# Where batch 2's projection and batch 1's values stand in a gated cross-attention and mixture kernel

## The chip, the cores and the metric

The kernel runs on one core of a Trainium2 chip. The metric is device time in microseconds (us) of one execution of the whole program. A profiled execution leaves a page and a trace; its span is the time from its first to its last recorded instruction.

Each core has engines with queues of their own, each worked off in order: TensorE (PE, matrix products; its weight loads are shown as PEld), VectorE (DVE), ScalarE (ACT), GpSimd (POOL) and SyncE (SP), which here only issues DMAs. What one engine needs from another, it waits for on semaphores.

## The reference

Eight batches of 256 tokens with 512 features go through two blocks. All of it is float32.

```python
# x, ctx_2048: (8, 256, 512)
h = layernorm(x)
q = heads([ctx_2048, h] @ Wq, 32)          # 32 query heads of 16
k, v = heads(h @ Wk, 8), heads(h @ Wv, 8)  # 8 key and value heads
ks, vs = heads(ctx_2048 @ Wsk, 8), heads(ctx_2048 @ Wsv, 8)
scores = q @ [ks, k].T / 4 + alibi         # each of the two key halves:
scores[masked] = -inf                      # causal, the last 64 keys
x = x + tanh(g_xattn) * (softmax(scores) @ [vs, v] @ Wo)

t = layernorm(x)
probs = softmax(t @ w_router)              # 128 experts, the 4 best
basis[k] = silu(t @ w_gate[k]) * (t @ w_up[k])       # 8 bases of 256
mixed = sum over the 4 experts of their mix of the 8 bases
shared = (silu(t @ shared_w_gate) * (t @ shared_w_up)) @ shared_w_down
x = x + tanh(g_ffn) * (mixed @ w_down + shared)
```

## The kernel before

**Three kinds of work.** For each batch there are the projection, the attention with a tail for each of its two tiles of 128 tokens, and the feed-forward block. While the feed-forward of batch b runs, the attention of batch b + 1 and the projection of batch b + 2 run between its matmuls.

**The order is written by hand.** Each kind of work is a Python generator which emits some instructions and yields a cost. `start(gen, length, at, total)` enters one with a time at which it begins and the stretch over which its costs are spread. `run` (L1252) always continues the generator that is earliest by this clock. The clock exists only while the program is built: it settles in which order instructions enter each engine's queue. A unit of it is one batch. Batch 0's attention begins at -0.585, its feed-forward at about 0, the projection of batch 2 at -0.06 with a length of 0.62, that of batch b + 2 for the later b at b + 0.01 (L1265 to L1285).

**Projection.** `project(b)` (L507) loads the input `x` and the context (`ctT`, stored with features as rows) where b > 1, normalises on VectorE (`norm`), transposes the normalised tiles on PE (`tr_x`, result `xnT`), makes keys (`pk`, copied by ScalarE in four pieces to `kT`, L572), queries in four groups of eight matmuls (`pq`, four with `ctT`, four with `xnT`; each group copied to `qT` by ScalarE, L593), and values (`pv`, copied to `vpad` by `put_values`, L501). `pk`, `pq` and `pv` share one PSUM bank (`ps_one`, tag "one"), which a generator takes with `hold` and gives back with `give`. In `project(1)` the transposes go to another bank and no input is loaded, since it comes at the program's start.

**Values for the attention.** `diagonals(qd, eng)` (L491) issues four DMAs which copy a quarter of `vpad` to its place in `vbd`, the stationary operand of the value products (L731). There is one `vpad` and one `vbd` for all batches. Sixteen such DMAs make one batch's `vbd`. In `attention(b)` for b > 0 they go out on SP's queue at the steps `u` 1 and 2, mixed with the softmax.

**Attention.** A score group `i` (eight of them) has two softmax steps `u`. `score(i)` emits the score matmuls (L652), `soften` (L665) reads a block of scores on VectorE, adds the bias and finds the largest, `exponentials` (L684) is on ScalarE, `divide` (L693, L696) takes a reciprocal on VectorE and multiplies on GpSimd, `turn` (L709) transposes on VectorE, `values` (L731) multiplies with `vbd` on PE, `take` copies to `oT` on ScalarE. `tail(b, t, oT)` (L866) does the output projection (`po`), the sum with x and its norm, the transposes `tr_f`, the router (`pl`, the four best, `pst`, `pc`). The feed-forward of a batch begins when both tiles' `tr_f` are in `hT` and VectorE has formed sums of token tiles (`sT`).

**Batch 0's attention carries other work.** `first_batch` (L752) emits softmax and products of batch 0, and between them, by `piece(...)`, steps of a list of remaining projection work: `rest()` (L437) and behind it `project(1)`. A `piece` names the kinds of step which it may take: `BEFORE` and `MORE` are matmuls, `AFTER` is a copy out of PSUM. What is left at the end runs as `others()`.

**Feed-forward.** `feed_forward(b)` (L999) has ten pieces k: eight bases and two halves of the shared expert. Each is computed as seven block products of half size instead of eight (Strassen's way: sums of token tiles and of weight blocks), `m` at L1028 and L1037. The sums of weight blocks are formed once, in batch 0, by `sub` on VectorE and GpSimd, and written by `keep` to a scratch in HBM; later batches load them from there. For the pieces 0 to 2 this happens in `first_weights` (L269) and `first_sums`, before batch 0's feed-forward; for the pieces from 3 on inside its loop, one piece ahead. `after(i, g)` issues, when the last matmul that reads a weight buffer has been emitted, the load of the piece two further on. SP's queue carries all of these: weight loads, `vbd` copies, inputs and scratch writes, in the order in which they were emitted.

Of the kernel before, what the change touches and what calls it, by code (L numbers as in the profile page):

```python
# [15 lines left out]
P = 128  # L16
B, T, HID = 8, 256, 512
# [5 lines left out]
Q = 32  # L23
# [14 lines left out]
def gated_block(  # L38
# [23 lines left out]
    nc = tc.nc  # L62
# [45 lines left out]
    loaded = {}  # L108
# [160 lines left out]
    def first_weights():  # L269

        for k in (2, 0, 1):
            for g in range(1, 5):
                load_gu(k, g)
            if k == 2:
                yield 2.0
                later["wd"] = weight(w_down, I, HID, "wd", nc.sync)


                later["sd"] = sd = const.tile([P, NSI // 2, HID], F32, tag="sd", name="sd")
                nc.sync.dma_start(  # L280
                    sd, sw_down.rearrange("(j o p) n -> o p j n", o=2, p=P)[1]
                )
            if k == 0:
                yield 5.5
                yield from first_sums(2)
        yield 1.0
        yield from first_sums(0)
        yield 1.0
        yield from first_sums(1)
# [217 lines left out]
    def project(b, xns=None):  # L507
        def own():
            yield from hold(0.0 if b == 1 else GAP)

        def bank(shape, name):
            return ps_one.tile(shape, F32, tag="one", name=name)

        free = give
        if b > 1:
            while b > 2 and b - 3 not in stored:
                yield 0.5
            loaded[b] = load(b), load_context(b)
            yield 16.0
        xt, ctT = loaded[b]  # L520
        if xns is None:
            normed = norm(xt, range(NT), f"a{b}")
            yield 3.0
            xns = normed()
            yield 3.0
        xnT = two.tile([P, NC, T], F32, tag="xo", name=f"xnT_{b}")
        kT = two.tile([P, 2, 2, T], F32, tag="kT", name=f"kT_{b}")

        def keys(pk, s):
            w_sb, src = ((wsk_sb, ctT), (wk_sb, xnT))[s]  # L530
            for c in range(NC):
                nc.tensor.matmul(  # L532
                    pk[:, s, :], lhsT=w_sb[:, c, :], rhs=src[:, c, :],
                    start=(c == 0), stop=(c == NC - 1),
                )

        if b == 1:

            yield BEFORE
            yield from own()  # L540
            pk = bank([P, 2, T], f"pk_{b}")
            for t in range(NT):
                if t:
                    yield BEFORE
                    keys(pk, 0)
                    yield MORE
                evict = transposed(
                    xnT, xns[t], t, f"x{b}",
                    lambda shape, name: other_bank(2, name).rearrange("p (c n) -> p c n", n=P),
                )  # L550
                yield AFTER
                evict()
            yield BEFORE
            keys(pk, 1)
            yield AFTER
        else:
            for t in range(NT):
                yield from own()
                evict = transposed(xnT, xns[t], t, f"x{b}", bank)
                yield AFTER - 0.8  # L560
                evict()
                free()
                yield BEFORE + 0.8
            yield from own()
            pk = bank([P, 2, T], f"pk_{b}")
            for s in range(2):
                keys(pk, s)
                yield AFTER

        for par in range(2):  # L570
            for s in range(2):
                nc.scalar.activation(  # L572
                    kT[:, par, s, :], pk[:, s, :], AF.Copy, scale=kmask[:, par : par + 1],
                )
        free()
        yield BEFORE
        if b == 1:
            yield BEFORE


        qT = two.tile([P, NB, G, Q], F32, tag="qT", name=f"qT_{b}")
        for g in range(G):
            yield from own()
            pq = bank([P, T], f"pq_{b}_{g}")
            for c in range(2 * NC):
                nc.tensor.matmul(  # L586
                    pq, lhsT=wq_sb[:, c, g * P : (g + 1) * P],
                    rhs=(ctT if c < NC else xnT)[:, c % NC, :],
                    start=(c == 0), stop=(c == 2 * NC - 1),
                )  # L590
                if c % NC == NC - 1:
                    yield MORE if c < NC else AFTER
            nc.scalar.activation(  # L593
                qT[:, :, g, :], pq.rearrange("p (b q) -> p b q", q=Q), AF.Copy, scale=-0.25
            )
            free()
            yield BEFORE
        projected[b] = kT, qT


        yield from own()
        pv = bank([P, NT, 2, HK * D], f"pv_{b}")
        for t in range(NT):
            for s, (w_sb, src) in enumerate(((wsv_sb, ctT), (wv_sb, xnT))):
                for c in range(NC):
                    nc.tensor.matmul(  # L606
                        pv[:, t, s, :], lhsT=src[:, c, t * P : (t + 1) * P], rhs=w_sb[:, c, :],
                        start=(c == 0), stop=(c == NC - 1),
                    )
            yield AFTER if t else MORE  # L610
        put_values(pv)
        free()
        yield BEFORE


    def attention(b):
# [135 lines left out]
        def first_batch():  # L752

            scs = {0: score(0)}
            for u in range(2 * n + 3):
                i, j = divmod(u, 2)
                m = u // 4 - 1 if u >= 6 and u % 4 == 2 else None
                if m is not None:

                    into = scs.get(i - 1) or [bank(f"sc_{b}_{i}_{p}") for p in range(2)]  # L760
                    values(m, 0, pts[m], into)
                exponentials()
                if i < n:
                    nmax = memory(u)
                if m is None:
                    piece(BEFORE, MORE)
                yield 1.0
                for step, ps in enumerate(((2,), (3,), (0, 1))):
                    exponentials()
                    for p in ps:  # L770
                        if i < n:
                            soften(i, j, p, scs[i], prs[u], nmax, dens[u])
                    if step == 0 and m is not None:
                        values(m, 1, pts[m], into)
                        piece(BEFORE, MORE)
                    if step == 1:
                        if j == 1 and i + 1 < n:
                            assert i + 1 < n // 2 or "queries" in ready
                            if i + 1 in (3, 7):
                                piece(AFTER)  # L780
                                piece(BEFORE, MORE)
                            scs[i + 1] = score(i + 1)
                        if 0 <= u - 1 < 2 * n:
                            divide((u - 1) // 2, (u - 1) % 2, prs[u - 1], dens.pop(u - 1))
                    if step == 2:
                        if 0 <= u - 2 < 2 * n:
                            turn(u - 2)
                        if m is not None:
                            take(m, into)
                            if m == n // 4 - 1:  # L790
                                start(tail(b, 0, oT), 0.22, total=37.0)
                        piece(AFTER)
                    yield 1.0 if i < n else 0.3
            start(tail(b, 1, oT), 0.16, total=37.0)
            start(others(), 1.0, total=100.0)
            yield 0.1

# [7 lines left out]
        for u in range(2 * n + 4):  # L805
# [12 lines left out]
            yield 1.0  # L818

            for step, ps in enumerate(((2,), (3,), (0, 1))):  # L820
                if u in (1, 2) and step < 2:
                    diagonals(2 * (u - 1) + step, nc.sync)
                exponentials()
                for p in ps:
# [442 lines left out]
    start(after_diagonals(), 0.2, at=-0.535, total=1.0)  # L1267
    start(first_weights(), 0.39, at=-0.537, total=20.5)
    start(attention(1), 0.86, at=FIRST, total=74.1)
    at = -0.2  # L1270
    while 0 not in sides:
        at += 0.005
        run(at)
    for b in range(B):
        if b > 0:
            run(b + EARLY)
            if b + 1 < B:
                start(attention(b + 1), 0.86, at=b + EARLY, total=74.1)
            run(float(b))
            at = float(b)  # L1280
        start(feed_forward(b), b + 1.0 - at, at=at, total=72.9)
        if b + 2 < B:
            start(project(b + 2), 0.62, at=b + (0.01 if b > 0 else -0.06), total=60.0)
    run(float(B + 1))


# [37 lines left out]
```

## Time and profile before

| | |
|---|---|
| three timed runs | 1010.71, 1011.7, 1012.34 us; median 1011.7 |
| the profiled execution | 1013.49 us, span 1011.7 us, mean clock of PE 0.993 |
| HBM read and written | 158.87 MB, 14.68 MB |
| the chain that ended last | PE 86% of the span, DVE 5%, issue 2%, ACT 2%, POOL 2% |
| first feed-forward matmul of batch 0 | 88.9 us |

How to read it: the page gives busy time for each engine as a share of the span. "The chain that ended last" is followed back from the program's last instruction, at each step to what released it, and says on which engine the time lay. The table of waits names, for each kind of instruction of an engine, what ended the idle time before it: `PE sc L731 <- DVE nm L665: 5.3, 1, 5.3` is 5.3 us in total, one time, the longest 5.3, in which PE stood before a value product that VectorE's `soften` released. "issue" as releaser means that nothing which the profile shows was awaited. In a timeline a line is start and duration, engine, line of the kernel, operation, out<-in, shape, and in brackets the wait before it. Tables by window give for each stretch of time the busy time of PE, PEld, DVE, ACT and POOL with the number of instructions, and of SP, then the clock that PE was granted as a share of full speed, the busy share of the DMA engines and GB/s.

### The profile page before, as it was taken

Reading aid. Unit: us, or ns where it says so; the run is one execution under the profiler, and the core shown is the slowest. Engines: PE = TensorE matmul, PEld = TensorE weight load, DVE = VectorE, ACT = ScalarE, POOL = GpSimd, SP = SyncE. Lnnn points to the kernel's source line nnn. Section 1 sums busy time; section 2 is a strip of 40 time slices with the busy share of each in tenths; the row PEclk is TensorE's granted clock in tenths of the full one; section 3 lists DMA queues with packets and bytes.
Section 4 is the critical chain, followed back from the end, with each engine's and each line's share of the span. In section 5 each row is a group of like instructions: output and inputs, shape, how many; then the busy total and the mean of one; then the engine's idle time right before and its main releaser. Section 6 shows DMA issues by size and latency. Waiting matters only on the chain.

```text
span 1011.7 us, 27844 instructions
## 1 busy us (share of the span) xinstructions
PE 985.7 (97%) x10470; PEld 797.3 (79%) x10470; DVE 601.8 (59%) x2241; ACT 441.6 (44%) x1657; POOL 471.6 (47%) x892
## 2 busy tenths in 40 slices
PE   8899799899999999999999999999999999999998
PEld 8777687768888687886778868797788868787885
DVE  2775767467553685536755467645756466665453
ACT  3754444246442564325543356423554245442231
POOL 4783676536542363423634246432455325651341
PEclk9999899999999999999999999999999999999999
DMA  6945744689354784457745586446954468665891
GB/s 208 219 171 155 224 152 129 185 216 304 124 164 144 208 288 142 147 166 217 249 127 158 167 256 216 135 137 190 276 188 140 150 181 260 201 192 167 281 301 64
DMA packets 117302, 192.15 MB, mean 190 GB/s; under 512 B 12848, under 2 KB 34864, under 8 KB 117168
## 3 DMA queue, kind: packets, MB, share of 16 engines
q1 hardware_dynamic: 112672, 184.87, 59.6%
q10 hardware_dynamic: 4112, 4.46, 1.3%
q8 instruction: 83, 1.36, 0.6%
q0 software_dynamic: 384, 1.05, 0.5%
q14 instruction: 51, 0.42, 0.1%
HBM read 158.87 MB, written 14.68 MB: 172 GB/s over the span
## 4 chain that ended last, share of the span: by engine, by line
PE 86%; DVE 5%; issue 2%; ACT 2%; POOL 2%; DMA 1%; SPq 1%; ACTq 0%; DVEq 0%; POOLq 0%
PE m L1028 39%; PE m L1037 10%; PE pq L586 8%; PE sc L731 6%; PE po L893 5%; PE sc L652 5%; PE pd L1171 4%; PE pk L532 2%; PE pv L606 2%; PE pd L1174 2%; PE pl L923 1%; DVE pr L665 1%; ACT pr L684 1%; PE tr_x L204 1%; SPq L496 1%
## 5 line engine op out<-in xcount | busy, mean ns | idle before, releaser
L696 POOL TENSOR_SCALAR pr<-pr,rd 128x192 f32<-128x192 f32 (+2 forms) x512 | 212.1, 434 | 243.9 <-DVE rd L693 226.8
L684 ACT ACTIVATE pr<-pr,nm 128x192 f32<-128x192 f32 (+2 forms) x512 | 219.0, 431 | 106.7 <-DVE nm L665 55.3
L1028 PE MATMUL m<-w,sT 128*128 128x256 f32 x1024 | 252.3, 380 | 1.3 <-issue 0.8
L1028 PEld LDWEIGHTS m<-w,sT 128*128 128x128 f32 x1024 | 193.6, 190 | 28.9 <-issue 1.5
L665 DVE CUSTOM_DVE_ANT_1 pr<-sc,nbias 128x192 f32<-128x192 f32 (+2 forms) x512 | 153.7, 321 | 98.0 <-PE sc L652 91.1
L1028 PE MATMUL m<-w,hT 128*128 128x256 f32 x768 | 203.8, 388 | 1.0 <-DVE u L1073 1.0
L1028 PEld LDWEIGHTS m<-w,hT 128*128 128x128 f32 x768 | 139.6, 191 | 25.6 <-issue 6.3
L1118 POOL TENSOR_TENSOR mixed<-mixed,th 128x256 f32<-128x256 f32 x112 | 81.5, 728 | 137.5 <-DVE th L1113 137.5
L709 DVE STREAM_TRANSPOSE pt<-pr 128x768 f32<-128x768 f32 (+2 forms) x128 | 111.4, 870 | 3.8 <-POOL pr L696 3.1
L684 ACT ACTIVATION_READ_ACCUMULATOR pr<-pr,nm 128x1 f32 x512 | 98.0, 191 | 0.0
L1074 POOL TENSOR_TENSOR m<-m,u 128x256 f32<-128x256 f32 x80 | 61.4, 768 | 67.3 <-DVE u L1073 58.5
L990 ACT ACTIVATE th<-m 128x256 f32<-128x256 f32 x80 | 30.7, 384 | 138.5 <-DVE up L1084 138.4
L731 PEld LDWEIGHTS sc<-pt,vbd 64*32 64x32 f32 x5120 | 60.6, 106 | 25.8 <-issue 14.2
L731 PE MATMUL sc<-pt,vbd 64*32 64x64 f32 (+2 forms) x5120 | 68.2, 228 | 8.9 <-DVE nm L665 5.3
L1096 DVE TENSOR_TENSOR gate<-u,m 128x256 f32<-128x256 f32 x80 | 33.2, 416 | 72.0 <-PE m L1028 66.5
L1084 DVE TENSOR_TENSOR up<-u,m 128x256 f32<-128x256 f32 x80 | 33.3, 416 | 67.9 <-PE m L1028 41.1
L990 ACT ACTIVATE th<-gate 128x256 f32<-128x256 f32 x80 | 33.3, 416 | 76.5 <-DVE gate L1096 76.5
L652 PE MATMUL sc<-kT,qT 32*128 32x192 f32 (+2 forms) x1024 | 63.6, 336 | 2.8 <-DVE nm L665 2.5
L1037 PE MATMUL m<-sT,w 128*128 128x128 f32 x512 | 66.2, 278 | 0.0
L652 PEld LDWEIGHTS sc<-kT,qT 32*128 32x128 f32 x1024 | 44.3, 184 | 26.5 <-issue 7.1
L1037 PEld LDWEIGHTS m<-sT,w 128*128 128x128 f32 x512 | 62.3, 194 | 0.4
L1171 PE MATMUL pd<-sd,shT 128*128 128x512 f32 x128 | 61.5, 603 | 0.2 <-DVE shT L1107 0.2
(131 smaller groups left out, 1376.0 us busy)
## 6 DMA issues: line engine op xcount, KB each, us to landing
w<-s SPq DMA_DIRECT2D x284, 256.0 KB, 3.5
w<-in_L_ffn_w_gate SPq DMA_DIRECT2D x130, 256.0 KB, 3.1
w<-in_L_ffn_w_up SPq DMA_DIRECT2D x73, 256.0 KB, 4.1
vbd<-vpad SPq DMA_DIRECT2D x120, 128.0 KB, 3.1
s<-w SPq DMA_DIRECT2D x40, 256.0 KB, 3.3
w<-in_L_ffn_shared_w_gate SPq DMA_DIRECT2D x32, 256.0 KB, 2.9
w<-in_L_ffn_shared_w_up SPq DMA_DIRECT2D x18, 256.0 KB, 3.8
sd<-in_L_ffn_shared_w_down SPq DMA_DIRECT2D x16, 256.0 KB, 3.5
```

Source lines behind the costliest of these rows:

```text
L586: nc.tensor.matmul(pq, lhsT=wq_sb[:, c, g * P : (g + 1) * P], rhs=(ctT if c < NC else xnT)[:, c % NC, :], start=(c == 0), stop=(c == 2 * N ...
L652: nc.tensor.matmul(seen(scs[p][:, j * COLS : (j + 1) * COLS], qb), lhsT=qT[rows, qb].rearrange("p g q -> p (g q)"), rhs=kT[rows, par, :, f ...
L665: nc.vector.tensor_tensor_reduce(out=part, in0=seen(scs[p][:, j * COLS : (j + 1) * COLS], qb0 + j), in1=bass.AP(tensor=bias.tensor, offset ...
L684: nc.scalar.activation(part, part, AF.Exp, bias=nmax, scale=-1.0, accum_out=den)
L696: nc.gpsimd.tensor_scalar(part, part, rden[:, p : p + 1], 1.0, op0=ALU.mult, op1=ALU.mult)
L709: nc.vector.transpose(pt[:, u % 4].rearrange("p c (s k) -> p (c s) k", s=2)[:, :, lo:], pr.rearrange("p c (s k) -> p (c s) k", s=2)[:, :, ...
L731: nc.tensor.matmul(scs[gp][32 * c : 32 * (c + 1), 2 * COLS + lo * Q : 2 * COLS + hi * Q], lhsT=vbd[rows, kb % (P // Q), kb // (P // Q) * 2 ...
L990: nc.scalar.activation(th, gate, AF.Tanh, scale=0.5)
L1028: nc.tensor.matmul(dst, lhsT=sides_of[m][c], rhs=w[:, c, :], start=(first and c == 0), stop=(c == NC // 2 - 1), skip_group_check=True,)
L1037: nc.tensor.matmul(dst[:, cols], lhsT=w[:, c, cols], rhs=sides_of[m][c], start=(first and ic == c == 0), stop=(c == NC // 2 - 1), skip_gro ...
L1118: nc.gpsimd.tensor_add(mixed[t], mixed[t], th)
L1171: nc.tensor.matmul(po, lhsT=shT[:, ic, t * P : (t + 1) * P], rhs=down[ic], **flags)
```

## The change

Six edits, of which none adds or removes a computation:

- `first_weights` loads batch 2's `x` and `ctT`, behind the weight loads of its last piece. `project(2)` then doesn't load them.
- The values of a batch become a function of their own, `project_values`. For batch 1 it is called ahead of the queries, for later batches behind them, as before.
- `first_batch` takes no `piece` of matmuls at step 9.
- Batch 1's sixteen `vbd` copies are issued on SP at the end of `first_batch`, in place of steps 1 and 2 of `attention(1)`.
- `project(2)` starts at -0.2 with a length of 0.75 (before: at -0.06, 0.62).
- The loop no longer starts `project(2)`; the projections of batches 3 to 7 start as before.

```diff
@@ first_weights
             if k == 0:
                 yield 5.5
                 yield from first_sums(2)
+        loaded[2] = load(2), load_context(2)
         yield 1.0
         yield from first_sums(0)
@@ project
         if b > 1:
             while b > 2 and b - 3 not in stored:
                 yield 0.5
-            loaded[b] = load(b), load_context(b)
-            yield 16.0
+            if b not in loaded:
+                loaded[b] = load(b), load_context(b)
+                yield 12.0
+            yield 4.0
         xt, ctT = loaded[b]
...
         yield BEFORE
         if b == 1:
             yield BEFORE
+            yield from project_values(b, ctT, xnT, bank, own, free)
+            ready.add("values")
...
         projected[b] = kT, qT
+        if b > 1:
+            yield from project_values(b, ctT, xnT, bank, own, free)
+
+    def project_values(b, ctT, xnT, bank, own, free):
         yield from own()
         pv = bank([P, NT, 2, HK * D], f"pv_{b}")
         for t in range(NT):
...
         put_values(pv)
         free()
         yield BEFORE
@@ first_batch
                 if i < n:
                     nmax = memory(u)
-                if m is None:
+                if m is None and u != 9:
                     piece(BEFORE, MORE)
...
             start(tail(b, 1, oT), 0.16, total=37.0)
+            assert "values" in ready
+            for qd in range(P // Q):
+                diagonals(qd, nc.sync)
             start(others(), 1.0, total=100.0)
@@ attention, batches from 1 on
             for step, ps in enumerate(((2,), (3,), (0, 1))):
-                if u in (1, 2) and step < 2:
+                if b > 1 and u in (1, 2) and step < 2:
                     diagonals(2 * (u - 1) + step, nc.sync)
@@ the schedule
     start(attention(1), 0.86, at=FIRST, total=74.1)
+    start(project(2), 0.75, at=-0.2, total=60.0)
     at = -0.2
     while 0 not in sides:
...
         start(feed_forward(b), b + 1.0 - at, at=at, total=72.9)
-        if b + 2 < B:
-            start(project(b + 2), 0.62, at=b + (0.01 if b > 0 else -0.06), total=60.0)
+        if 0 < b < B - 2:
+            start(project(b + 2), 0.62, at=b + 0.01, total=60.0)
```

## The prediction

> **What bounds the kernel now.** I read the engines' busy time first, then who TensorE waited for, then the clock by window, then the timeline around each wait.
>
> ```profile
> PE 985.7 (97%) x10470; PEld 797.3 (79%) x10470; DVE 601.8 (59%) x2241; ACT 441.6 (44%) x1657; POOL 471.6 (47%) x892
> ```
>
> TensorE (PE) is busy 985.7 of 1011.7 us, and the change neither adds nor removes a matmul. Only PE's idle time and time at half clock can move. The instruction orders of the two programs differ from batch 0's second half of attention to the end of batch 0's feed-forward (about 43 to 225 us) and nowhere later, so only waits before 225 us count. They are, in that view (us in total, times, longest):
>
> ```profile
> PE sc L731 <- DVE nm L665: 5.3, 1, 5.3
> PE sc L731 <- issue: 3.3, 1, 3.3
> PE pk L532 <- ACT xnT L205: 1.8, 1, 1.8
> ...
> PE pq L586 <- ACT kT L572: 0.8, 1, 0.8
> ...
> PE m L1028 <- DMA w<-in_L_ffn_w_up: 0.5, 1, 0.5
> PE pq L586 <- ACT qT L593: 0.5, 1, 0.5
> ```
>
> The clock comes on top. In the table by windows (the first figure after the window's length is PE's busy time, PEclk is near the end) a window with PE busy for 47% or less is followed by one at 0.50, one at 60% is not:
>
> ```profile
> 41.54:44.95 3.41, 1.59 (x22) 1.13 (x22) 3.27 (x15) 3.19 (x14) 2.86 (x8) 1.00 0.95 220
> 44.95:48.37 3.42, 3.42 (x8) 2.29 (x8) 2.26 (x11) 1.57 (x8) 3.42 (x8) 0.50 1.13 217
> ...
> 188.30:191.73 3.43, 2.06 (x89) 1.42 (x75) 2.30 (x11) 0.19 (x1) 2.29 (x4) 1.00 0.97 244
> 191.73:195.14 3.41, 1.50 (x45) 1.46 (x46) 1.42 (x3) 0.66 (x3) 0.73 (x1) 1.00 0.38 141
> 195.14:198.55 3.41, 3.41 (x18) 3.41 (x18) 0.94 (x2) 0.54 (x2) 0.44 (x1) 0.50 0.51 153
> ```
>
> So a hole of some 1.8 us in one window costs up to 1.7 us more (3.41 at half).
>
> **What the change takes away.** Before, SP issues twelve of the sixteen `vbd` copies, `x` and `ctT` between 91.69 and 103.6, ahead of the first weights of piece 3. These start at 103.67, land late, and VectorE, which must subtract them, stands still with batch 1's softmax queued behind it:
>
> ```profile
> 103.67 0.47 SPq L349 DMA_DIRECT2D w<-in_L_ffn_w_gate  x1
> ...
> 111.97 0.69 DVE L980 TENSOR_TENSOR w<-w,w 128x512 f32<-128x512 f32 x1 [3.27 <-DMA w<-in_L_ffn_w_gate]
> ...
> 117.01 1.55 PE L731 MATMUL sc<-pt,vbd 64*32 64x96 f32 x64 [5.25 <-DVE nm L665]
> ```
>
> Afterwards these eighteen DMAs are issued earlier: `x`, `ctT` behind the loads of piece 1 (some 59 us, while the queues are under 40% busy from 60 to 80 us), the copies from the end of batch 0's last value products on, 16 at about 0.64 = 10 us of SP, before piece 2's reload needs SP. Piece 3's loads then leave as soon as piece 1's matmuls free their buffers, and batch 2's projection (21 us of PE work) stands between pieces 0 and 5, so PE has work while VectorE subtracts. Gone: 5.25 + 0.48, and half clock from 117.0 to 120.05, 1.5: **-7.2**. The 0.8 before `pq` at 134 us shrinks, since two more groups cover `kT`: between -0.8 and 0, nearest -0.5.
>
> The 3.28 us "issue" hole at 190.36 lies inside a run of equal matmuls and waits for no engine; a 16 KB packet of the instruction queue moved at 191.4, among 380 GB/s of other traffic. With its half-clock window (195.14 to 198.55) it costs 3.28 + 1.7 = 5.0. It stands at a fixed place in PE's stream, in the second half of batch 1's last value products. In the new order about 1.8 us of other matmuls (two runs of L1037) come between the halves instead of 0.9. Bounds: it stays (0) or goes (-5.0); nearer to going, as twice the cover is there: **-3.6**. The Trainium skill (Runtime: NRT & Kernel Launch, Instruction fetch mechanics) says that crossing a 16 KiB block of instructions is mostly hidden; this hole was not, and by the rule the term would be -5.0.
>
> **What it adds.** Batch 0 first. `u` counts softmax steps, two to a score group. (1) The key matmuls `pk<-xnT` move behind score group 5 and the value products. Gone are 1.82 of wait and the half-clock 3.68 against 1.73 for eight such matmuls. But group 5's banks are free only when VectorE has read step 9's first two blocks (45.4), and the value products need the transpose that ends at 47.3: PE idles 2.3 + 1.1, with 0.5 of half clock. `pk` ends at about 51.0; the same work was done before at 50.8: **+0.2** (up to +1.7 if the clock falls twice).
>
> (2) The hole that decides. ScalarE's order is now exp 10 (two), `oT`, the four `kT` copies, exp 10 (two). The last wait for `kT`, hence for `pk` at 51.0: 1.6 + 1.0 + 0.1 = 53.7, and VectorE's reciprocal of step 10 with all behind it waits there, as it did at 53.19 before:
>
> ```profile
> 53.19 0.17 DVE L693 RECIPROCAL rd<-dn 128x4 f32<-128x4 f32 x1
> ...
> 62.09 0.34 DVE L665 CUSTOM_DVE_ANT_1 pr<-sc,nbias 128x192 f32<-128x192 f32 x1
> ...
> 63.12 0.93 PE L652 MATMUL sc<-kT,qT 32*128 32x192 f32 x16
> ```
>
> From there to step 13's first block VectorE worked without a break for 8.9 us; its order is unchanged, so step 13 begins at 62.6. Before, PE had three halves of query products to do meanwhile (57.0 to 63.1). Now it has `po` (3.4), score 6 (0.9) and `pv` (3.6), done at 59.0; then come `pq<-ctT` in the one bank that `pv` holds. The copy of `pv` to `vpad` stands on ScalarE behind the first exp of step 13: 62.6 + 0.4 + 0.7 + 0.6 = 64.4. PE idles 5.4 us (5.0 to 5.5), with score 7 and the rest of batch 0 queued behind it, and starts at half clock: 4.4 us of it on the windows above, 2.0 lost (1.7 to 3.4). **+7.4**.
>
> (3) Three times a second query group follows the first with nothing between, at 0.47 each (the row of `pq <- qT`), once before: **+0.9** (0.5 to 1.4).
>
> (4) From `po` of the second tile to `tr_f` VectorE and GpSimd need 4.1 us (82.42 to 86.55); PE now has 2.15 to do in it: idle 1.95 against 1.66 before (0.73 + 0.26 + 0.67): +0.3. In one piece it may cost a window: 0 or 1.7, the middle 0.8. **+1.1**.
>
> (5) VectorE has batch 2's norm (two statistics 1.8, two normalisations 1.4 to 2.9) in the same order, behind `xn_f` and ahead of the router's top-4. `rest`, which `pst` of tile 1 transposes, is then ready some 8.1 us after `xn_f`; PE is there after 2.4 (`tr_f`, score, `pl`) + 3.5 = 5.9, and all matmuls of piece 0 queue behind: 2.3 (1.9 to 2.8) and a window of 0 to 1.7, taken at 1.0. **+3.3**.
>
> (6) Without projection, pieces 5 to 7 have 11.1 + 8.6 + 8.1 = 27.8 us of PE work by the rows' durations, against 28.4 on VectorE and 28.3 on GpSimd. Before, projection filled them. Piece 6 alone lacks 1.3. Bounds 0 (batch 1's piece 2 ran in 7.27 us with VectorE busy 6.97) and 3.2; taken **+1.6**.
>
> The Trainium skill (TensorE: Matmul & The Clock Gate, Why this matters for your kernels) warns of PE gaps over about 3 us only. The windows above show half clock after gaps of 1.8 and 1.9. By the rule the 0.8 and 1.0 of (4) and (5) fall away, and the sum would be 1.8 less.
>
> Sum: 0.2 + 7.4 + 0.9 + 1.1 + 3.3 + 1.6 = 14.5 added; 7.2 + 0.5 + 3.6 = 11.3 removed: **+3.2 us**. The profiled execution took 1013.49 with a span of 1011.7; the timed runs' median is 1011.7 too, so the sum is put on that: 1014.9.
>
> **The rivals.** *The early hole is not there*: the softmax runs ahead by the 2.1 us that group 5 starts earlier, and `vpad` is copied before PE needs it. For: VectorE waited 2.10 for group 5 at 49.37. Against: `kT` on ScalarE. Then (2) falls: 3.2 - 7.4 = -4.2, 1007.5; with the fetch hole quite gone 1006. Chance 0.31. *All cancels*: fetch hole gone (-1.4), no half window in (4) and (5) (-1.8), (6) hidden (-1.6): -1.6, 1010.1. Chance 0.18. *The late pieces bind too*: fetch hole stays (+3.6), (6) at 3.2 (+1.6): +8.4, 1020. Chance 0.12. *The 111 us stall stays*, since VectorE had 29.5 us of work for PE's 25 there, and not the loads alone bound it: +7.2, 1022. Against: PE's pieces 1 to 3 grow to 38.5 us of work. Chance 0.04.
>
> **Numbers.** The forecast itself has 0.35, its own range 1013 to 1019. Slower by over 0.2% (2.0 us, about what a measurement of this kernel can tell from no change): 0.35 + 0.12 + 0.04 = 0.51. Within: 0.18. Faster: 0.31. The range takes in the first rival to 1006 and the third at 1020.
>
> **What would show it.** Right: PE idle some 5 us before `pq<-ctT` near 59 us, released by ScalarE's `vpad`; a PE wait of 2 us at `pst` on VectorE's `rest`; piece 0's first matmul some 9.6 us later than 88.87; no wait on a weight's DMA near 120; few idle gaps to 180. Wrong: first feed-forward matmul before 93, or the hole under 2 us; then the first rival holds. A hole in pieces 5 to 7 over 4 us, or a stay of the fetch hole, makes it worse than 1019.

## The result and the profile after

The changed kernel's four timed runs took 1016.51 to 1018.71 us, median 1017.89; four of the kernel before took 1010.71 to 1012.34, median 1011.91. The ratio is 1.0071, 95% interval 1.005 to 1.0092: slower, by about 6 us. The profiled execution of the changed kernel took 1016.51 us with a span of 1014.7.

The two profiled spans are only 3.0 us apart. The first trace of before is one of its longer executions: a second one (run e1) has a span of 1008.9. All programs here are the same up to batch 1's first key products. These begin at 39.65 in the first trace of before, at 38.45 in the second and at 38.41 in that of after, so the readings below are against the second: +5.8 us of span from an equal start.

First the page's line of busy time of the changed kernel, then who TensorE waited for from 40 to 232 us, that is to the end of batch 0's feed-forward (us in total, times, longest).

```profile
PE 984.0 (97%) x10470; PEld 795.3 (78%) x10470; DVE 598.3 (59%) x2241; ACT 441.8 (44%) x1657; POOL 471.4 (46%) x892
```

```profile
PE pq L591 <- ACT vpad L503: 3.9, 1, 3.9
PE tr_f L204 <- DVE xn_f L190: 3.2, 2, 2.2
PE sc L661 <- DVE nm L674: 2.6, 3, 1.9
PE pst L969 <- DVE tsum L963: 2.2, 2, 1.9
PE sc L740 <- DVE pt L718: 1.9, 2, 1.6
PE m L1040 <- ACT prob L946: 1.6, 1, 1.6
PE sc L740 <- issue: 1.5, 1, 1.5
PE pq L591 <- ACT qT L598: 1.4, 3, 0.5
```

The work is the same. The two long waits of before (5.3 near 112 us, 3.3 without a releaser near 190) are gone, and the eight kinds above stand in their place. Batch 0's first feed-forward product, in the second trace of before and in after:

```profile
86.33 1.03 PE L1028 MATMUL m<-w,hT 128*128 128x256 f32 x4
```

```profile
97.43 1.03 PE L1040 MATMUL m<-w,hT 128*128 128x256 f32 x4
```

From the first key products to this product after takes 97.43 - 38.41 = 59.0 us, before 86.33 - 38.45 = 47.9, so **+11.1**. From there to batch 1's first feed-forward product it takes 133.5 against 138.3: **-4.8**. The rest, 783.8 against 784.3, has the same order of instructions. Against the first trace, from which the prediction was worked out, the two stretches are +9.8 and -4.2 (49.2 and 137.6 there).

### The profile page after: what moved, and what is told of

The parts are those of the page before. It is cut to its first block, busy times and chain, and to the rows that moved or that the text cites. A ratio compares the mean times of both kernels' runs of the same rounds, so it can differ in the third digit from the quotient of the medians.

```text
span 1014.7 us, 27827 instructions
## 1 busy us (share of the span) xinstructions
PE 984.0 (97%) x10470; PEld 795.3 (78%) x10470; DVE 598.3 (59%) x2241; ACT 441.8 (44%) x1657; POOL 471.4 (46%) x892
## 4 chain that ended last, share of the span: by engine, by line
PE 85%; DVE 6%; DMA 3%; SPq 2%; ACT 1%; POOL 1%; issue 1%; ACTq 0%; DVEq 0%; POOLq 0%
PE m L1040 37%; PE pq L591 10%; PE m L1049 9%; PE sc L740 6%; PE po L905 5%; PE sc L661 5%; PE pd L1183 4%; PE pv L615 2%; PE pk L535 2%; PE pd L1186 2%; DMA x<-in_x 1%; SPq L497 1%; DMA wo<-in_L_xattn_Wo 1%; DVE pr L674 1%; PE pl L935 1%
## 5 line engine op out<-in xcount | busy, mean ns | idle before, releaser
L740 PE MATMUL sc<-pt,vbd 64*32 64x96 f32 (+2 forms) x5120 | 68.5, 229 | 3.7 <-DVE pt L718 1.9
```

The costliest lines, as they stand in the source:

```text
L740: nc.tensor.matmul(scs[gp][32 * c : 32 * (c + 1), 2 * COLS + lo * Q : 2 * COLS + hi * Q], lhsT=vbd[rows, kb % (P // Q), kb // (P // Q) * 2 ...
```

## The experiments

The last two columns are those two stretches in the profiled execution. Their sum follows the ratios roughly, and they say where a run gained or lost. They are of one execution: that of e9 took 1008.19 us, 2 below its median. In brackets is the median of the kernel before in the same comparison.

| run | median us | ratio to before, 95% | to first feed-forward product | batch 0's feed-forward |
|---|---|---|---|---|
| e1 before again | 1010.95 (1011.33) | 1.0003, 0.9986 to 1.002 | 47.9 | 138.3 |
| e2 early loads only | 1009.53 (1011.33) | 0.9983, 0.9967 to 0.9999 | 47.7 | 136.3 |
| after | 1017.89 (1011.91) | 1.0071, 1.005 to 1.0092 | 59.0 | 133.5 |
| e3 projection 2 late | 1016.92 (1011.33) | 1.0067, 1.0043 to 1.0091 | 59.4 | 132.0 |
| e4 values in one piece | 1010.22 (1011.33) | 0.9992, 0.9977 to 1.0006 | 51.7 | 133.9 |
| e5 copy one place earlier | 1013.98 (1011.2) | 1.0033, 1.002 to 1.0047 | 55.4 | 132.8 |
| e6 no skip at step 9 | 1009.17 (1011.2) | 0.9981, 0.997 to 0.9992 | 51.0 | 132.6 |
| e7 = e4, length 0.88 | 1006.16 (1011.2) | 0.9956, 0.9941 to 0.9972 | 51.2 | 130.1 |
| e8 = e4 and e6 | 1021.62 (1011.2) | 1.0097, 1.0073 to 1.012 | 58.5 | 137.9 |
| e9 = e6, projection 2 late | 1010.31 (1010.25) | 1.0, 0.9984 to 1.0016 | 51.0 | 132.2 |
| e10 = e6, length 0.88 | 1004.94 (1010.25) | 0.9954, 0.9939 to 0.9969 | 50.5 | 129.3 |
| e11 = e6, length 1.0 | 1006.74 (1010.25) | 0.9966, 0.9953 to 0.9979 | 51.2 | 130.7 |
| e12 = e10, vbd late | 1005.84 (1011.74) | 0.9945, 0.9924 to 0.9965 | 50.8 | 130.9 |

**e1, the kernel before once more.** No edit.

> The kernel before, once more, for a second trace. If the hole of 3.28 us without a releaser in the value products at 190 us belongs to that place in TensorE's stream, it is there again, with 1 to 4 us, and the time is 1011.9 within 0.1%. If it is chance, it is absent, and the span is 3 to 5 us below the 1011.7 of the first trace. The wait of 5.25 us near 112 is there in both cases.

The hole near 190 came again, with 2.72 us at the same matmul (37 of a run of 64 left), and the wait near 112 with 5.20. So the hole belongs to the place. What differed was the clock: a window at half clock at 45 us, which only the first trace has, and behind the hole two such windows in the second trace against one.

**e2, the early loads alone**, on the kernel before.

```diff
+        loaded[2] = load(2), load_context(2)
         yield 1.0
         yield from first_sums(0)
...
-            loaded[b] = load(b), load_context(b)
+            if b not in loaded:
+                loaded[b] = load(b), load_context(b)
             yield 16.0
```

> Before, with batch 2's x and ctT issued on SP some 40 us earlier, and no other instruction moved. My theory: the weights of piece 3 come late because twelve vbd copies stand ahead of them, and x and ctT are only the last two of fourteen; they move up by about 1.3 us, the wait near 112 shrinks from 5.25 to about 4, the time to 1010 to 1011.5. Rival: the two inputs' own traffic (1 MB) is what delays them: then the wait is under 1 us and the time 1004 to 1007.

The wait near 112 fell from 5.20 to 3.90: about the two DMAs' time on SP (102.35 to 103.67 in before), 2 of the 14 that stand ahead of the weights. The inputs' traffic is not the cause.

**e3, batch 2's projection at its old place**, on after.

```diff
-                yield 12.0
-            yield 4.0
+            yield 16.0
...
-    start(project(2), 0.75, at=-0.2, total=60.0)
...
-        if 0 < b < B - 2:
-            start(project(b + 2), 0.62, at=b + 0.01, total=60.0)
+        if b + 2 < B:
+            start(project(b + 2), 0.62, at=b + (0.01 if b > 0 else -0.06), total=60.0)
```

> After, but batch 2's projection starts where it did before; its early loads, the values ahead and the early vbd copies stay. My theory: the early vbd copies remove the wait near 112, and the early projection causes the new waits of TensorE at pieces 0 and 5 to 8 (1.6 before a feed-forward product at 101, 1.0, 0.2, 1.9 and 1.6 from 176 to 200). So the early hole of 3.9 stays, the 112 wait stays away, the late ones go: 6 to 7 us below after, 1010.5 to 1012. Rival: the projection's matmuls in pieces 0 to 5 are what covers VectorE's lag near 112; then a wait of 3 to 5 us comes back there and the time is 1015 to 1018.

Both were half right. The waits at 101 and from 176 to 200 shrank to 0.7 and less, but one of 1.61 came at 119 with a half-clock window behind it, and 0.8, 0.74 and 0.67 elsewhere. The stretch is 132.0 against 133.5, the time not measurably different from after. So the loss of 11 us in the first stretch has nothing to do with the early projection.

**e4, both tiles' value products in one piece**, on after.

```diff
-            yield AFTER if t else MORE
+            if t:
+                yield AFTER
+            elif b > 1:
+                yield MORE
         put_values(pv)
```

> After, but both tiles' value products of batch 1 in one piece, so that their copy stands on ScalarE between the exponentials of step 12, and not behind the first of step 13. My theory: the copy is done at about 59.4 instead of 62.6, TensorE's wait before the first query products falls from 3.9 to under 1, no half clock follows (1.7), the first feed-forward product comes at about 92.6 instead of 97.4, and of these 4.8 us VectorE's lag in pieces 5 to 8 takes 1 to 2 back: 1013.5 to 1015.5. Rival: VectorE and GpSimd set the end of batch 0's feed-forward; then all is given back, and the time stays at 1017 to 1018.

The wait fell from 3.86 to 0.68, the first stretch by 7.4 us, and only 0.4 of it came back later. The time fell by more than my theory said, since everything behind `pv` in the list moved up by one place: the three waits of 0.47 before query groups vanished too, and that before `tr_f` fell from 2.17 to 0.88.

**e5, the copy alone.** To separate the hole from that, one ScalarE instruction is moved by one place.

```diff
                 for step, ps in enumerate(((2,), (3,), (0, 1))):
+                    if u == 13 and step == 1:
+                        piece(AFTER)
                     exponentials()
```

> After, with one ScalarE instruction moved by one place: the copy of batch 1's values stands ahead of the first exponential of step 13 and not behind it; no other instruction moves on any engine. My theory: the copy then waits for the exponentials of step 12 only, which end at 60.1; TensorE's wait before the first query products falls from 3.9 to 1.9, and the time by 2, or by 3.4 if the half clock after it goes too: 1014 to 1016. Rival: the wait is paid again by the softmax chain behind it (VectorE idles 4.1 before score group 7 anyway): time unchanged at 1017 to 1018.5.

Timelines of after around the hole (start, duration, engine, line, operation; the wait before it in brackets), TensorE first, then ScalarE:

```profile
57.73 1.06 PE L615 MATMUL pv<-wv,xnT 128*128 128x128 f32 x8
62.65 1.67 PE L591 MATMUL pq<-ctT,wq 128*128 128x256 f32 x4 [3.86 <-ACT vpad L503]
```

```profile
59.99 0.19 ACT L693 ACTIVATION_READ_ACCUMULATOR pr<-pr,nm 128x1 f32 x1
61.43 0.45 ACT L693 ACTIVATE pr<-pr,nm 128x192 f32<-128x192 f32 x1 [1.25 <-DVE nm L674]
...
62.02 0.58 ACT L503 COPY vpad<-pv 128x512 f32<-128x512 f32 x1
```

and ScalarE and TensorE in e5:

```profile
60.33 0.18 ACT L693 ACTIVATION_READ_ACCUMULATOR pr<-pr,nm 128x1 f32 x1
60.42 0.56 ACT L503 COPY vpad<-pv 128x512 f32<-128x512 f32 x1
61.77 0.45 ACT L693 ACTIVATE pr<-pr,nm 128x192 f32<-128x192 f32 x1 [0.79 <-DVE nm L674]
```

```profile
61.04 1.99 PE L591 MATMUL pq<-ctT,wq 128*128 128x256 f32 x8 [1.90 <-ACT vpad L503]
```

The products were done at 58.8. ScalarE was free at 60.2 but stood before an exponential whose largest score VectorE had not found; the copy could have run then. One place earlier the wait is 1.90, as expected to a tenth, the half clock behind it is gone, and so are 3.9 us of the time. The wait was not paid again.

**e6, the skip at step 9 undone**, on after.

```diff
-                if m is None and u != 9:
+                if m is None:
                     piece(BEFORE, MORE)
```

> After, but with the piece at step 9, so that batch 1's key products stand ahead of score group 5 as before. My theory: one wait of 1.8 for the transposed input takes the place of the 1.9 and 0.4 before score group 5 and the value products; the wait for vpad stays near 4; the first feed-forward product and the time stay within 1 us of after. Rival: the skip itself starves TensorE near 45 us, and costs the 1.7 of half clock there: then 2 to 3 us below after.

Both theories fell: the time is 1009.17, some 9 us below after and 0.2% below before. I had looked only at the key products, which the skip moves. But `piece` takes the next step of one list, so a skipped turn delays all that follows by one turn. ScalarE in e6:

```profile
57.62 0.44 ACT L693 ACTIVATE pr<-pr,nm 128x192 f32<-128x192 f32 x1
...
58.68 0.58 ACT L503 COPY vpad<-pv 128x512 f32<-128x512 f32 x1 [0.53 <-PE pv L615]
```

and TensorE, which in after had waited 3.86:

```profile
59.32 2.00 PE L591 MATMUL pq<-ctT,wq 128*128 128x256 f32 x8 [0.67 <-ACT vpad L503]
```

The copy stands behind two exponentials of step 12 and waits for the products themselves. From that copy on, e6 and e4 have the same order on all engines. So with the values ahead it is `u != 9` that puts the copy behind the exponential. The line alone doesn't make the hole, since e4 keeps it and waits 0.68. The skip without the values ahead was not run.

**e7, e4 with a longer projection.**

```diff
-    start(project(2), 0.75, at=-0.2, total=60.0)
+    start(project(2), 0.88, at=-0.2, total=60.0)
```

> The kernel with the values in one piece, and batch 2's projection spread over a length of 0.88 instead of 0.75, so that it reaches into pieces 6 and 7. My theory: the waits of TensorE between 165 and 200 (1.3, 0.6, 1.8 and 1.8) come from pieces without projection; they fall to under 3 in all, with no new one over 1 near 115: 1 to 3 us below the kernel with one piece. Rival: the waits only move forward into pieces 2 to 4, as when the projection began late: same time within 1.5.

The waits from 165 to 200 fell from about 5.6 to 4.1, not to under 3, and none came near 115. The stretch is 3.8 us shorter than in e4, the time 4. Beside the 1.5 of the waits, 1.7 of this is a window at half clock at 91 us, which the trace of e4 has and that of e7 has not.

**e8, e4 and e6 together**, two turns gained instead of one.

> The kernel with the values in one piece, and batch 1's key products ahead of score group 5 again. My theory: the value products then stand ahead of the output projection, their copy is done before 57 on ScalarE, the waits for vpad (0.7) and before score group 5 (1.9) go, a wait of 1.8 for the transposed input comes back, and one query half more is done before score group 7: 1 to 3 us below the kernel with one piece, about 1008. Rival: VectorE sets the pace of the softmax there, and the time stays the same within 1.

Here the theory failed badly: 1021.62, the slowest of all. ScalarE and TensorE:

```profile
62.65 0.46 ACT L696 ACTIVATE pr<-pr,nm 128x192 f32<-128x192 f32 x1 [1.25 <-DVE nm L677]
...
63.10 0.36 ACT L598 ACTIVATE qT<-pq 128x256 f32<-128x256 f32 x1
```

```profile
63.52 0.80 PE L591 MATMUL pq<-ctT,wq 128*128 128x256 f32 x1 [2.29 <-ACT qT L598]
```

It is the same hole, with the next tenant of the one bank: now the copy of the first query group stands behind the first exponential of step 13. Half clock follows, waits of 2.46 and 3.21 before `tr_f`, and a hole of 2.31 without a releaser at 203.

**e9, e6 with the projection at its old place** (the edit of e3 on e6).

> After with the piece at step 9 and with batch 2's projection where it was before: what is left of the change are the values ahead, the early vbd copies and the early loads. It prices the early projection without the hole near 59 us. My theory: without it the waits from 165 to 200 (5.5 in all in the kernel with the piece at step 9) fall to some 2.5, and a wait of 1.6 near 120 with its half clock comes in: 1007.5 to 1010.5, within 1.5 of the kernel with the piece at step 9 (1009.2). Rival: the early projection is what keeps the wait near 112 away; then 1012 to 1014.

TensorE before batch 1's value products in e9, and all engines from 106.15 to 117.65:

```profile
116.65 1.16 PE L739 MATMUL sc<-pt,vbd 64*32 64x96 f32 x64 [2.56 <-DVE nm L673]
```

```profile
106.15:117.65 11.50, 8.94 (x173) 7.17 (x171) 11.21 (x44) 5.79 (x26) 7.74 (x13) 1.00 0.61 183
```

VectorE (third pair) waits for no weight any more but is busy for 11.21 of 11.50 us, batch 2's norm among it, and TensorE waits 2.56 for it. So the 5.2 near 112 had two halves: late weights, and VectorE's load. The early loads (e2) and vbd copies take away the first, the early projection the second, since e6 has no wait there. On balance e9 and e6 can't be told apart (their intervals overlap): with a length of 0.75 the early projection gives back in late waits what it gains here.

**e10 and e11, e6 with lengths 0.88 and 1.0.**

> After with the piece at step 9 and a length of 0.88 for batch 2's projection. My theory: both gains add, since they lie in different stretches: 4 us less than with the piece at step 9 alone, 1004.5 to 1006.5, the same as with the values in one piece. Rival: the gain of the length came from where the pieces of that one kernel fell: 1008 to 1010.

> The same with a length of 1.0: the projection reaches into pieces 7 and 8, and less of it stands in pieces 1 to 4. My theory: the waits from 165 to 200 shrink by another 1 to 2, but VectorE's lag near 115 shows as a wait of 1 to 2 of TensorE: 1004 to 1008, near the length of 0.88. Rival: later is simply better, and it falls below 1003.

Both gains add in e10, the lowest median; by their ratios e7, e10 and e12 can't be told apart. Who TensorE waited for in e10, 40 to 230 us, the longest four:

```profile
PE pk L535 <- ACT xnT L205: 1.8, 1, 1.8
PE sc L740 <- DVE nm L674: 1.6, 1, 1.6
PE pst L969 <- DVE tsum L963: 1.4, 1, 1.4
PE sc L740 <- issue: 1.3, 1, 1.3
```

No wait is over 2. At 1.0 the late waits are one of 2.70 at 186.6, and the wait forecast near 115 did not come; the intervals of the two overlap.

**e12, e10 with the vbd copies at their old place.**

```diff
-            for qd in range(P // Q):
-                diagonals(qd, nc.sync)
...
-                if b > 1 and u in (1, 2) and step < 2:
+                if u in (1, 2) and step < 2:
```

> The fastest so far (the piece at step 9, length 0.88) with one edit of the change undone: the sixteen vbd copies are issued in steps 1 and 2 of batch 1's attention again, among the weight loads; no other instruction moves. It asks whether the early copies matter once the projection is early. My theory: half of the wait near 112 was late weights (VectorE's 3.3 for a DMA), and these come back: TensorE waits 1 to 3 us more between 100 and 125, 1006 to 1009. Rival: with projection between pieces 0 and 5 TensorE has work to cover them: 1004 to 1005.5, and the early copies are worth nothing there.

The rival holds. VectorE waits for a weight again, but TensorE doesn't wait for VectorE there. VectorE's wait in e12:

```profile
DVE w L990 <- DMA w<-in_L_ffn_w_up: 1.1, 1, 1.1
```

Ratios 0.9945 and 0.9954 cannot be told apart: with the projection early, the early copies are worth nothing measurable.

## Why the prediction was right, and where not

The sign and the main reason were right: a hole before `pq<-ctT`, released by `vpad`, and the first feed-forward product 11.1 us later (9.6 forecast; 9.8 against the first trace). The sum was 3 us too low, and that the time still fell into the range of 1013 to 1019 is in part luck: the terms (1), (6) and a hole at 70 us came out 7 us higher than forecast, the terms removed and (2), (4) and (5) 6.5 us lower, and 2.4 us are in no term. Its terms, in its numbering, measured in after against the second trace of before:

| term | forecast | measured | |
|---|---|---|---|
| wait near 112 and half clock | -7.2 | -7.5 | 5.20, and 4.7 us of products at half clock |
| `pq` behind `kT` | -0.5 | -0.8 | gone |
| hole without a releaser at 190 | -3.6 | -5.9 | 2.72, and about 6.3 us at half clock |
| (1) keys moved | +0.2 | +2.5 | 12.15 against 11.46 up to `po`, with a query half (1.83) less done |
| (2) hole before `pq` | +7.4 | +5.6 | 3.86, and 3.41 us at half clock |
| (3) query groups | +0.9 | +0.9 | three waits of 0.47 against one |
| (4) second `tr_f` | +1.1 | +0.5 | 2.17 against 1.67, no half clock |
| (5) second tile's router | +3.3 | +2.1 | 1.59, 0.32 and 0.23, no half clock |
| (6) pieces without projection | +1.6 | +5.0 | 0.99, 0.25, 1.93, 0.23 and 1.56 from 175 to 200 |
| fetch hole at 70 | none | +1.5 | 1.51 |

These add up to +3.9; the stretch up to batch 1's feed-forward measured +6.3. The other 2.4 us lie in batch 0's feed-forward, most of it as time in which TensorE counts as busy with the same products, 0.6 of it with score products. Why is not settled.

**(1)** was sized on the first trace, whose window at half clock (44.95 to 48.37) the sum counts as gone. The second trace has none there. Against the first the term is +1.0 (12.96 up to `po`), and in after a whole window at half clock, from 46.04 to 49.46 with 1.7 lost, stands against the 0.5 of the sum.

**(2)** The mechanism is shown by e5, and its order on ScalarE was read rightly. The size was too large because step 13 came at 60.96 and not at 62.6. VectorE began at 53.23 and not at 53.7, and I took its 8.9 us from there over from before: seven small instructions took 1.2 us less, the first 0.15 (at 53.32) against 0.90 (at 53.28). What the step lacked was that, with the values ahead, the skip makes the hole: e6 without the skip is 9 us faster, and e8, with one turn more still, has the hole again.

**(6)** is the step that failed in size: +1.6 with an upper bound of 3.2, and +5.0 measured. I summed each engine's work per piece and let the fullest set the pace. What TensorE met were chains: its own turn comes, and the item it needs is queued on VectorE behind feed-forward work. VectorE ahead of the longest of the waits, 1.93 at 192.01:

```profile
191.96 1.11 DVE L992 TENSOR_TENSOR w<-w,w 128x512 f32<-128x512 f32 x1
193.00 0.80 DVE L962 TENSOR_TENSOR rest<-prob,rest 128x128 f32<-128x128 f32 x1
193.72 0.14 DVE L963 TENSOR_SCALAR tsum<-tsum 128x1 f32<-128x1 f32 x1
```

A weight difference of 1.11 us stands in front of the router's last steps. By e7 against e4 and e10 against e6, the longer projection is worth 3 to 4 us, of which some 1.5 each time are these late waits.

**(5)** was right in cause, but the wait came one item earlier, at a feed-forward product whose bank the router's scores still held (released by ScalarE's `prob`), and the clock did not fall. In e3, without batch 2's norm there, that wait did not come.

Of the two gaps which the prediction read from its windows for (4) and (5), 1.8 and 1.9, the second is only the part in its window of the wait of 3.28. After the waits of 2.17 and 1.59 no half clock followed, so the 1.8 us that the sum held for it in (4) and (5) did not come.

**The removed terms** hold. The reason for the first was half the story, as e9 shows. The hole at 190 went, as forecast; whether the matmuls between the halves covered it or the waits that TensorE now has just before (1.93 and 1.56) is not shown. A hole of the same kind came at 70, which no term had:

```profile
68.74 1.14 PE L740 MATMUL sc<-pt,vbd 64*32 64x32 f32 x95
71.39 0.21 PE L740 MATMUL sc<-pt,vbd 64*32 64x32 f32 x1 [1.51 <-issue]
```

**The rivals.** "The early hole is not there" came true in e4 and e6, at 1010.2 and 1009.2 instead of the 1007.5 worked out for it. In after itself the third one came true in its parts, a hole without a releaser (though elsewhere) and (6) above its upper bound of 3.2; with (2), (4) and (5) smaller than forecast the time stayed below its 1020. Of "all cancels" the hole at 190 and the missing half clock in (4) and (5) came true, but (6) was not hidden.

## What to carry to other kernels

Where one PSUM bank passes from product to product, the copy that empties it should be placed by what stands ahead of it on the copying engine: behind an instruction that still waits for a third engine, it holds TensorE for that wait as well. Where work is dealt out from one list, a skipped turn moves everything behind it; look at the order of each engine's queue, not at the item that the edit names. And filler work taken from a late stretch uncovers the chains there, so spread it (here a length of 0.88) rather than only start it earlier.

## What was new about the hardware

**Half clock.** The prediction read that windows of 3.41 us with TensorE busy for 47% or less are followed by one at half clock. Two windows and their followers, in e5 and in e10:

```profile
59.18:62.59 3.41, 1.55 (x7) 1.40 (x8) 3.41 (x17) 2.27 (x9) 2.26 (x4) 1.00 0.84 258
62.59:66.00 3.41, 3.41 (x172) 2.65 (x176) 2.94 (x11) 1.99 (x9) 3.41 (x7) 1.00 0.63 223
```

```profile
83.41:86.82 3.41, 1.78 (x23) 1.26 (x22) 2.70 (x8) 0.89 (x3) 3.09 (x3) 1.00 0.86 194
86.82:90.24 3.42, 3.13 (x11) 2.88 (x12) 2.98 (x14) 1.26 (x6) 1.02 (x3) 0.50 0.76 208
```

45% was followed by full clock, 52% by half, so the busy share alone doesn't decide. The first window held query products of 128x128 weights, the second score blocks of 32 rows, transposes and small router products. Whether the kind of product decides was not tried. Over all fourteen traces, 36 to 226 us, there are 743 windows at full clock: the 19 with TensorE busy for 1.52 us or less were all followed by half clock, of 45 with 1.55 to 2.23 it was 11, and of the others none. The longest wait near the second window was 0.89 us. The Trainium skill (TensorE: Matmul & The Clock Gate, Why this matters for your kernels) names only gaps of over about 3 us as dangerous; here the measurement decides, and shorter ones cost a window too. Two plain cases are the wait of 1.82 in the first trace of before and one of 1.91 before score group 5 in e5, each inside one window with half clock behind it.

The same wait of 1.8 us before `pk` at 42 to 45 us was followed by half clock in the first trace of before and not in the second, where a window's edge at 43.24 divides it. Nine traces have this wait: in before and e11 it lies whole in one window and half clock follows, in e1, e2, e6, e8, e9, e10 and e12 an edge divides it and none follows. This agrees with the same page (Part 1: The HAM clock gate), which says that the window of 3413 ns runs freely and is not started by the kernel. So for waits of 1 to 2 us a term for half clock is a matter of chance here.

**Holes without a releaser** of 0.9 us or more stand at a fixed place of TensorE's stream: at 190 us with 2.7 to 3.3 in before, e1 and e2, and at 66 to 72 with 0.9 to 1.5 in after and e3 to e12, each inside a run of short value products; e8 has a second one of 2.31 at 203. In after, a 16 KB packet of the instruction queue moved from 69.03 to 69.96, and TensorE went on at 71.39. At each of these fifteen holes it went on 1.2 to 1.5 us after the end of such a packet. The place is a count: the early hole stands behind the 857th matmul in all eleven traces that have it, the late one behind the 2251st, in e8 behind the 2255th. In before the 857th is a query product, and there is no hole. So an edit that changes which products stand at such a count moves a hole in or out, some 1 to 3 us either way. That TensorE waits for the packet's instructions there is inferred from these times.
